# Values' 1x1 products moved ahead of the first convolution, and a fifth buffer of attention weights, in layer 0 of a four-layer network

## The chip, the cores and the metric

The kernel runs on one core of a Trainium2 chip. Its time is the device time in microseconds from the first to the last instruction of the launch, and lower is better. The time before the change is the median of three runs, 4035.57 us (4034.29 to 4037.03).

## The reference, cut to what matters

The network has four layers on x of shape 2 x 128 x 64 x 64 (two samples, 128 channels, 4096 positions), each in the form x + f(groupnorm(x)). Only layer 0 is touched:

```python
xn = biasfree_ln(x, ln1_w)
qkv = conv1x1(xn, w_qkv)                       # 128 -> 5 * 128 channels
qkv = conv3x3_depthwise(qkv, w_dw)             # one 3x3 filter per channel
q1, k1, v, q2, k2 = jnp.split(qkv, 5, axis=1)  # then cut into 4 heads of 32 channels
q1, q2, k1, k2 = map(l2norm_tokens, (q1, q2, k1, k2))
attn1 = softmax(einsum('bhnc,bhmc->bhnm', q1, k1) * temperature)  # 4096 x 4096 per head
out1 = einsum('bhnm,bhmc->bhnc', attn1, v)
attn2 = softmax(einsum('bhnc,bhnd->bhcd', q2, k2) * temperature)  # 32 x 32 per head
out2 = einsum('bhnc,bhcd->bhnd', v, attn2)
out = conv1x1(out1 + out2, w_po)
out = conv1x1(biasfree_ln(out, ln2_w), w_proj) + b_proj
```

## The kernel before, in words

Channels lie on the 128 partitions, positions along the free dimension; everything is float32. Layer 0 (`_layer0`) normalizes the first sample and then does, for each sample b, `convolutions` and `attention`; the end of a sample, `finish` (output products, second normalization, residual), is a generator that runs inside the next sample's convolutions. `_in_order` ties every engine to the order in which the program is written, so the order of the Python statements is the order of each engine's queue. A list written out by hand sets the order around the change.

**Convolutions.** A group (q1, k1, v, q2, k2) is treated in two halves of 32 rows. For each half, `pointwise` (L1586 on) does the 1x1 product: POOL sets the frame's borders to zero (L1588, L1589, L1591), TensorE makes five pieces (L1597), ScalarE copies them from PSUM into a frame of 34 x 66 (four copies, L1604). The 3x3 depthwise filter follows in one of two ways:

- on TensorE (`depthwise`, L1619): 144 products of 32 x 32 blocks with diagonal weights, into two pairs of PSUM banks. This is used for q1, q2, k2 and half 1 of k1: seven blocks n = 0 to 6, in the list `order`. q1 and k1 are then copied by `in_place` (L1639), eight copies each on ScalarE and VectorE; q2 and k2 by `copy` (L1630), one on each engine, into a tile "qk". ScalarE takes sums of squares (L1644).
- on VectorE (`taps`, L1654 and L1656): nine steps over the whole half, one for each tap. This is used for half 0 of k1 and both halves of v: 27 steps. They are dealt out between the blocks by a tuple, one number for each block and one tuple for each sample: (5, 5, 5, 4, 4, 4, 0) for the first, (2, 6, 6, 4, 4, 4, 0) for the second; one more is done ahead.

After block n, `pointwise` for block n + 2 follows on TensorE. The values' `pointwise` are called by `values_of` after blocks 0 and 2. Frames of k1 half 0 and of v share a ring "vpad" of two. After block 2 the norms of q1 and k1 give a scale "sc" (L1766), with which VectorE scales q1 after block 3 (L1770). `products` (L1684, L1694) multiplies q2 by k2 after blocks 4 and 6 (by token, after transposes, copied as "tok" by L1630), `value_tiles` (L1668) turns v after blocks 5 and 6. In the second sample, six of the steps of the first sample's `finish` come after block 0 and the rest after block 1.

**Attention.** There are 8 sweeps (one for each 512 queries) of 32 tiles (128 keys). For each tile TensorE makes scores for four heads (L1858), ScalarE takes the exponential, one bank (L1930) and then three (L1933), into a tile "weights", TensorE multiplies the weights by v two tiles later (L1850), and VectorE adds the weights into running sums (L1881). Four tiles of each sweep start a sum and need no add. A tile of weights is free for ScalarE when both have read it; the ring has four buffers for the first sample and five for the second. At a sweep's end, totals are copied (L1899), turned (L1907) and divided into the result (L1913 to L1916). In the first sample the total and its turned form have tiles of their own, in the second they lie in a tile that is no longer needed. One step in every four tiles goes to side work: the channel attention (whose input is the tile "own", L1775, and the product's copy "folded", L1795), and in the first sample the normalization of the second (tiles "gn", L1545, and "y", L1526).

Of the kernel before, what the change touches and what calls it, by code (L numbers as in the profile page):

```python
# [10 lines left out]
F32 = mybir.dt.float32  # L11
# [5 lines left out]
B, C, H, W = 2, 128, 64, 64  # L17
S = H * W
CH = 512
# [1435 lines left out]
def _layer0(ctx, tc, X, a, cst, worst, there, dram):  # L1455
    nc = tc.nc
    one = ctx.enter_context(tc.tile_pool(name="f0_one", reuse_waits="tile", bufs=1))
    small = ctx.enter_context(tc.tile_pool(name="f0_small", reuse_waits="tile", bufs=2))
# [43 lines left out]
    v = one.tile([128, S], F32, name="v")  # L1502
# [80 lines left out]
    def frame(pool, tag="pad", bufs=2):  # L1583
        return pool.tile([128, H // 2 + 2, W + 2], F32, tag=tag, name=tag, bufs=bufs)

    def pointwise(pad, grp, half):  # L1586

        nc.gpsimd.memset(pad[:, :, 0:1], 0.0)  # L1588
        nc.gpsimd.memset(pad[:, :, W + 1 : W + 2], 0.0)  # L1589
        edge = 0 if half == 0 else H // 2 + 1  # L1590
        nc.gpsimd.memset(pad[:, edge, :], 0.0)  # L1591
        first, to = (0, 1) if half == 0 else (H // 2 - 1, 0)
        for r0, n in ((4 * ROWS, 1), (0, ROWS), (ROWS, 2 * ROWS), (3 * ROWS, ROWS)):
            ps = sp() if n > ROWS else acc(int(r0 == 0)).rearrange("p (o c) -> p o c", o=1)
            for i in range(0, n, ROWS):
                rows = min(ROWS, n - i)
                nc.tensor.matmul(  # L1597
                    ps[:, i // ROWS, : rows * W],
                    w_qkv[:, grp * C : (grp + 1) * C],
                    xn[:, (first + r0 + i) * W : (first + r0 + i + rows) * W],  # L1600
                    start=True,
                    stop=True,
                )
            nc.scalar.copy(  # L1604
                pad[:, to + r0 : to + r0 + n, 1 : W + 1],
                ps.rearrange("p k (h w) -> p (k h) w", w=W)[:, :n, :],
            )
            yield
# [37 lines left out]
    def taps(grp, half, to, pad):  # L1646

        cols = slice(half * S // 2, (half + 1) * S // 2)
        out = to[:, cols].rearrange("p (h w) -> p h w", w=W)
        for t in range(9):  # L1650
            x = pad[:, t // 3 : t // 3 + H // 2, t % 3 : t % 3 + W]
            tap = wd[:, 9 * grp + t : 9 * grp + t + 1]
            if t == 0:
                nc.vector.tensor_scalar_mul(out, x, tap)  # L1654
            else:
                nc.vector.scalar_tensor_tensor(out, x, tap, out, ALU.mult, ALU.add)  # L1656
            yield
# [45 lines left out]
    def convolutions(pool, b, before):  # L1703


        ss = small.tile([128, 2, 4], F32, tag="ss", name="ss")
        ss2 = small.tile([128, 2, 4, 2], F32, tag="ss2", name="ss2")
        gram = None
        order = [(1, 1), (0, 0), (0, 1), (3, 0), (4, 0), (3, 1), (4, 1)]
        kpad = frame(pool, "vpad")  # L1710
        run(pointwise(kpad, 1, 0))
        first = taps(1, 0, k1, kpad)
        frames = [frame(pool) for _ in range(2)]
        run(pointwise(frames[0], *order[0]))
        next(first)
        run(pointwise(frames[1], *order[1]))
        by_vector = first

        def values_of(half):
            pad = frame(pool, "vpad")  # L1720
            run(pointwise(pad, 2, half))
            return taps(2, half, v, pad)

        qk = None
        for n, (grp, half) in enumerate(order):
            ps = depthwise(grp, frames.pop(0))
            following = iter(())
            if n + 2 < len(order):
                frames.append(frame(pool))
                following = pointwise(frames[-1], *order[n + 2])  # L1730
            if grp >= 3:
                if grp == 3:
                    qk = pool.tile([128, 2, 4, CH], F32, tag="qk2", name="qk2", bufs=1)
                for p in range(2):
                    copy(qk[:, grp - 3, 2 * p : 2 * p + 2, :], ps[p])
                run(following)
                for r in range(4):
                    squares(pool, qk[:, grp - 3, r, :], ss2[:, grp - 3, r, half : half + 1])
            else:
                out = (q1, k1)[grp]  # L1740
                in_place(ps, half, out, 0)
                next(following, None)
                in_place(ps, half, out, 1)
                run(following)
                squares_of(pool, out, half, ss[:, grp, :])
            if n == 0:
                by_vector = chain(by_vector, values_of(0))
                for _ in range(FIRST_PART):
                    next(before, None)
            elif n == 1:  # L1750
                run(before)
            if n == 4:
                gram = acc(1)
                run(products(pool, qk, 0, gram))
            elif n == 5:
                run(value_tiles(0))
            elif n == 6:
                run(value_tiles(1))
                run(products(pool, qk, 1, gram))
            if n == 2:  # L1760
                squares_of(pool, k1, 0, ss[:, 1, :])
                by_vector = chain(by_vector, values_of(1))
                nq = inverse_norm(ss[:, 0, :], "nq1")
                nk = inverse_norm(ss[:, 1, :], "nk1")
                sc = small.tile([128, 1], F32, tag="sc", name="sc")
                nc.vector.scalar_tensor_tensor(sc, nq, nk, temp, ALU.mult, ALU.mult)  # L1766
            if n == 3:
                for c in range(0, NCH, 2):
                    cols = slice(c * CH, (c + 2) * CH)
                    nc.vector.tensor_scalar_mul(q1[:, cols], q1[:, cols], sc)  # L1770
            for _ in range(((5, 5, 5, 4, 4, 4, 0), (2, 6, 6, 4, 4, 4, 0))[b > 0][n]):
                next(by_vector, None)

        own = small.tile([128, 4, C], F32, tag="own", name="own", bufs=1)
        nc.vector.tensor_mul(  # L1775
            own,
            gram.rearrange("p (r c) -> p r c", r=4),
            blocks.unsqueeze(1).to_broadcast([128, 4, C]),
        )
        return ss2, own  # L1780
# [58 lines left out]
    def attention(pool, b, side):  # L1839
# [62 lines left out]
        def normalized(qb, first, t):  # L1902
            cols = slice(qb * CH, (qb + 1) * CH)
            turned = xn[:, CH : 2 * CH].rearrange("p (n i) -> p n i", i=32)
            if b == 0:
                turned = pool.tile([128, CH // 32, 32], F32, tag="turned", name="turned", bufs=1)
            nc.vector.transpose(turned.rearrange("p n i -> p (n i)"), t)  # L1907
            if first:
                by_query[qb] = small.tile([128, CH // 32], F32, tag="first", name="first")
                nc.vector.tensor_copy(by_query[qb], turned[:, :, 0])  # L1910
                return
            rec = small.tile([128, CH // 32], F32, tag="rec", name="rec")
            nc.vector.tensor_add(rec, turned[:, :, 0], by_query.pop(qb))  # L1913
            nc.vector.reciprocal(rec, rec)
            nc.vector.transpose(turned, rec.unsqueeze(2).to_broadcast([128, CH // 32, 32]))
            nc.vector.tensor_mul(  # L1916
                q1[:, cols], q1[:, cols], turned.rearrange("p n i -> p (n i)")
            )

        for n in range(last + 1):  # L1920
            kt = n % NQT
            mine, other = 3 * (n % 2), 3 * ((n + 1) % 2)
            three = banks[:, mine : mine + 3, :]
            at["spare"] = [other, other + 1]
            held[n] = pool.tile([128, 4, CH], F32, tag="weights", name="weights", bufs=4 + b)
            scores(n, three)
            total = None
            if len(pending) == 2 and kt in (STARTS[-1] + 1, 1):
                total = totals(banks[:, other + 2, :])
            nc.scalar.activation(held[n][:, 0, :], single, AF.Exp)  # L1930
            if n % 4 == 3:
                next(side, None)
            nc.scalar.activation(held[n][:, 1:, :], three, AF.Exp)  # L1933
            if total:
                emptied(*total)
            if n > 1:
                multiply(n - 2)
            add(n)
            if totalled and kt < 2:
                normalized(*totalled.pop())  # L1940
# [52 lines left out]
    def run(gen):  # L1993
        for _ in gen:
            pass

    def chain(*gens):
        for g in gens:
            yield from g
# [590 lines left out]
```

## Time and profile before

| | us |
|---|---|
| median of the runs | 4035.57 |
| profiled execution, its own time | 4028.9 |
| its span | 4027.1 |
| first sample, convolutions (from the first 1x1 product to the first tile of scores in full flow) | 32.3 to 184.9 |
| first sample, attention | 187.4 to about 769 |
| second sample, convolutions with the first one's finish | 764.1 to 956.7 |
| second sample, attention | 959.2 to about 1517 |
| TensorE busy over the span | 3855.3 |
| VectorE busy over the span | 3198.8 |
| ScalarE busy over the span | 3242.4 |

The profile is one execution; its time is 6.7 us below the median of the runs. A row of a timeline gives the start, the time from the first to the last end of a merged group, engine, line, operation, output and inputs, shapes and count; in square brackets stands the idle time before it and what ended it. A row of waits gives who waited for whom, the total, the number of times and the longest. PE is TensorE, PEld its weight loads, DVE VectorE, ACT ScalarE, POOL GpSimd.

### The profile page before, as it was taken

The page shows a single profiled execution, that of the slowest core. Times are in us where ns is not written, and L with a number is a line of the kernel's source. Part 1 is how long each engine was busy: PE and PEld are TensorE (multiplying, and loading weights), DVE is VectorE, ACT ScalarE, POOL GpSimd, SP SyncE. Part 2 cuts the span into 40 slices and gives each one's busy share as a digit, 9 for nine tenths or more (in the row PEclk, how much of TensorE's full clock was granted, in tenths as well). Part 3 has the DMA queues.
Part 4 walks back from the last instruction along what each step waited for, and adds up shares of the span by engine and source line. Part 5 has one row for each costly group of instructions (what it writes and reads, how often), then busy time and mean ns, then how long its engine had stood idle before and what let it go on. Part 6 is the DMA issues. An engine that isn't in the chain of part 4 may idle for free.

```text
span 4027.1 us, 82181 instructions
## 1 busy us (share of the span) xinstructions
PE 3855.3 (96%) x35214; PEld 1323.1 (33%) x35214; DVE 3198.8 (79%) x3572; ACT 3242.4 (81%) x3955; POOL 79.5 (2%) x145
## 2 busy tenths in 40 slices
PE   7999999989999998997998999999999999999998
PEld 3511222344121114445664332332223222322222
DVE  6699999777999998996667787777777777776666
ACT  5488998736899993216645999999999999999998
POOL 1000000000000001000000000000000000000000
PEclk9999999999999999998998999999999999999999
DMA  1199960000000000004754110110002000110000
GB/s 51 27 197 189 189 95 1 2 2 2 2 2 2 2 2 13 6 3 175 298 217 131 40 40 27 46 53 30 27 24 74 30 27 25 43 48 6 6 6 4
DMA packets 193128, 217.59 MB, mean 54 GB/s; under 512 B 30441, under 2 KB 154345, under 8 KB 188658
## 3 DMA queue, kind: packets, MB, share of 16 engines
q1 hardware_dynamic: 192754, 212.25, 20.6%
q8 instruction: 278, 4.55, 0.5%
q14 instruction: 96, 0.79, 0.1%
HBM read 178.64 MB, written 98.57 MB: 69 GB/s over the span
## 4 chain that ended last, share of the span: by engine, by line
PE 68%; DVE 5%; issue 2%; ACT 1%; POOL 0%; SPq 0%; DMA 0%; POOLq 0%; DVEq 0%; ACTq 0%
PE ps_acc L2305 25%; PE ps_s L2282 18%; PE ps L1850 6%; PE ps L1858 6%; PE ps_bank L710 2%; PE ps_z L1008 2%; DVE e L950 2%; PE ps_t L640 1%; PE ps_bank L590 1%; PE ps_bank L1062 1%; PE ps_bank L681 1%; PE ps_acc L2209 1%; PE ps_acc L2163 1%; PE ps_pe L925 1%; DVE sums L1881 1%
## 5 line engine op out<-in xcount | busy, mean ns | idle before, releaser
L2296 ACT ACTIVATE weights<-ps_s 128x1024 f32<-128x1024 f32 x1920 | 1780.9, 1066 | 75.0 <-PE ps_s L2282 74.9
L2305 PE MATMUL ps_acc<-weights,vt 128*32 128x512 f32 x8192 | 1091.9, 605 | 0.0
L1881 DVE TENSOR_TENSOR sums<-sums,weights 128x2048 f32<-128x2048 f32 x384 | 854.9, 2285 | 7.8 <-ACT weights L1933 5.6
L2282 PE MATMUL ps_s<-q,k 64*128 64x512 f32 x4096 | 830.8, 470 | 3.5 <-DMA k<-stack 2.4
L1933 ACT ACTIVATE weights<-ps 128x1536 f32<-128x1536 f32 x512 | 740.7, 1447 | 8.5 <-PE ps L1858 8.5
L2282 PEld LDWEIGHTS ps_s<-q,k 64*128 64x128 f32 x4096 | 349.3, 184 | 934.3 <-ACT weights L2296 808.8
L1858 PE MATMUL ps<-q,k 32*64 32x512 f32 x8192 | 575.0, 613 | 12.5 <-ACT weights L1930 11.8
L1850 PE MATMUL ps<-weights,vt 128*32 128x512 f32 x4096 | 545.0, 604 | 0.0
L2254 DVE SCALAR_TENSOR_TENSOR exp_z<-exp_z,exp_m 128x1024 f32<-128x1024 f32 x384 | 469.0, 1221 | 9.3
L1930 ACT ACTIVATE weights<-ps 128x512 f32<-128x512 f32 x512 | 306.6, 599 | 88.3 <-PE ps L1858 33.5
L2238 DVE TENSOR_SCALAR exp_i<-ps_s 128x1024 int32<-128x1024 f32 x128 | 156.7, 1225 | 215.3 <-PE ps_s L2282 215.1
L1858 PEld LDWEIGHTS ps<-q,k 32*64 32x64 f32 x8192 | 120.6, 130 | 442.5 <-ACT weights L1930 393.4
L2305 PEld LDWEIGHTS ps_acc<-weights,vt 128*32 128x32 f32 x8192 | 162.4, 108 | 308.9 <-issue 308.1
L1850 PEld LDWEIGHTS ps<-weights,vt 128*32 128x32 f32 x4096 | 84.5, 108 | 391.1 <-issue 378.1
L662 DVE SCALAR_TENSOR_TENSOR X<-g,w,X 128x2048 f32<-128x2048 f32 x84 | 197.4, 2351 | 2.6
L1881 DVE TENSOR_TENSOR sums<-weights 128x2048 f32<-128x2048 f32 x64 | 145.8, 2289 | 32.7 <-ACT weights L1933 31.9
L2258 DVE SCALAR_TENSOR_TENSOR weights<-exp_z,exp_i 128x1024 f32<-128x1024 f32 x128 | 156.8, 1225 | 15.6 <-DVE exp_z L2254 0.5
L2254 DVE SCALAR_TENSOR_TENSOR exp_z<-exp_m 128x1024 f32<-128x1024 f32 x128 | 155.9, 1218 | 0.0
L1008 PE MATMUL ps_z<-w_ri,e 128*32 128x128 f32 x2048 | 137.5, 409 | 14.6 <-DVE e L950 12.4
L1619 PE MATMUL ps<-pad,diag 32*32 32x512 f32 x4032 | 144.0, 611 | 4.0 <-ACT vt L1630 3.7
L950 DVE TENSOR_SCALAR e<-ps_pe 32x136 f32<-32x136 f32 (+1 forms) x352 | 104.4, 297 | 4.9
L1619 PEld LDWEIGHTS ps<-pad,diag 32*32 32x32 f32 x4032 | 84.3, 104 | 59.3 <-issue 21.4
(310 smaller groups left out, 2955.6 us busy)
## 6 DMA issues: line engine op xcount, KB each, us to landing
w_ri<-w_r SPq DMA_DIRECT2D x16, 2112.0 KB, 7.9
w_ri<-w_i SPq DMA_DIRECT2D x16, 2112.0 KB, 13.5
stack<-qs SPq DMA_DIRECT2D x64, 256.0 KB, 2.1
q<-stack SPq DMA_DIRECT2D x128, 128.0 KB, 2.5
k<-stack SPq DMA_DIRECT2D x128, 128.0 KB, 2.6
stack<-ks SPq DMA_DIRECT2D x32, 256.0 KB, 2.2
w_r<-in_L_conv_kr_w SPq DMA_DIRECT2D x15, 528.0 KB, 12.6
w_r<-in_L_conv_kr_x SPq DMA_DIRECT2D x15, 528.0 KB, 12.8
```

What stands on the lines that cost most here:

```text
L662: nc.vector.scalar_tensor_tensor(xi, g[:, i : i + H // 2, j : j + W], w8[:, s : s + 1], xi, ALU.mult, ALU.add)
L1008: nc.tensor.matmul(out.rearrange("p (n f o) -> p n f o", n=2, f=2), e[:, s, 2 * j : 2 * j + 2, :].rearrange("p f x -> p (f x)"), w.rearran ...
L1619: nc.tensor.matmul(ps[r // 2][to, r % 2, :].rearrange("p (h w) -> p h w", w=W), diag[rows, grp, t, :], pad[rows, y0 : y0 + ROWS, t % 3 : t ...
L1850: nc.tensor.matmul(out[rows, :], lhs(rows), w[:, j, :], start=first, stop=stop)
L1858: nc.tensor.matmul(bank[64 * h : 64 * h + 64, :], k1[rows, kt * 128 + 64 * h : kt * 128 + 64 * h + 64], q1[rows, qb * CH : (qb + 1) * CH], ...
L1881: nc.vector.tensor_add(parts[p].rearrange("p j c -> p (j c)"), t.rearrange("p j c -> p (j c)"), w.rearrange("p j c -> p (j c)"),)
L1930: nc.scalar.activation(held[n][:, 0, :], single, AF.Exp)
L1933: nc.scalar.activation(held[n][:, 1:, :], three, AF.Exp)
L2254: nc.vector.scalar_tensor_tensor(z, x, n, m, ALU.add, ALU.mult)
L2282: nc.tensor.matmul(ps[j // 2][:, j % 2, :], g.k[kt // 4][rows, j // 2, keys], g.q[qb][rows, j // 2, :], start=True, stop=True,)
L2296: nc.scalar.activation(w[0], ps[p], AF.Exp)
L2305: nc.tensor.matmul(g.ac[32 * j : 32 * j + 32, :], g.vt[:, kt, j // 2, i : i + 2, :].rearrange("p a d -> p (a d)"), w[:, i, :], start=(at = ...
```

## The change

Both halves' 1x1 products of v now come before block 0, after those of k1 half 0 and of blocks 0 and 1, with two taps on VectorE after each of the four (eight ahead in all). The tuples that deal the taps are new. k1's frame lies in the ring of "qk" (which is first used at block 3), so the values' two frames have the ring "vpad" to themselves. The first sample's attention has five buffers of weights. To make room, "own" moves into the ring of "gn" (one buffer) and "turned" into the ring of "y" (two).

```diff
         order = [(1, 1), (0, 0), (0, 1), (3, 0), (4, 0), (3, 1), (4, 1)]
-        kpad = frame(pool, "vpad")
+        kpad = pool.tile([128, 8 * CH], F32, tag="qk2", name="kpad", bufs=1)
+        kpad = kpad[:, : (H // 2 + 2) * (W + 2)].rearrange("p (h w) -> p h w", w=W + 2)
         run(pointwise(kpad, 1, 0))
         first = taps(1, 0, k1, kpad)
         frames = [frame(pool) for _ in range(2)]
-        run(pointwise(frames[0], *order[0]))
-        next(first)
-        run(pointwise(frames[1], *order[1]))
-        by_vector = first
+        by_vector = [first]
+
+        def ahead():
+            for _ in range(2):
+                next(first)
 
         def values_of(half):
             pad = frame(pool, "vpad")
             run(pointwise(pad, 2, half))
-            return taps(2, half, v, pad)
+            by_vector.append(taps(2, half, v, pad))
+
+        for n in range(2):
+            run(pointwise(frames[n], *order[n]))
+            ahead()
+        for n in range(2):
+            values_of(n)
+            ahead()
+        by_vector = chain(*by_vector)
...
             if n == 0:
-                by_vector = chain(by_vector, values_of(0))
                 for _ in range(FIRST_PART):
...
                 squares_of(pool, k1, 0, ss[:, 1, :])
-                by_vector = chain(by_vector, values_of(1))
...
-            for _ in range(((5, 5, 5, 4, 4, 4, 0), (2, 6, 6, 4, 4, 4, 0))[b > 0][n]):
+            for _ in range(((3, 3, 3, 2, 4, 4, 0), (0, 2, 4, 4, 4, 5, 0))[b > 0][n]):
                 next(by_vector, None)
 
-        own = small.tile([128, 4, C], F32, tag="own", name="own", bufs=1)
+        own = cp.tile([128, 4, C], F32, tag="gn", name="own", bufs=1)
...
-                turned = pool.tile([128, CH // 32, 32], F32, tag="turned", name="turned", bufs=1)
+                turned = cp.tile([128, CH // 32, 32], F32, tag="y", name="turned")
...
-            held[n] = pool.tile([128, 4, CH], F32, tag="weights", name="weights", bufs=4 + b)
+            held[n] = pool.tile([128, 4, CH], F32, tag="weights", name="weights", bufs=5)
```

## The prediction

> **What bounds the kernel now.** I read the page first, then the TensorE, VectorE and ScalarE timelines of the two convolution stages (32 to 183 us for the first sample, 764 to 955 us for the second), then busy times by stretch and the waits of the two attention stages between and after them. The page says that the whole is a TensorE chain, so what counts is where TensorE stands still.
>
> ```profile
> PE 3855.3 (96%) x35214; PEld 1323.1 (33%) x35214; DVE 3198.8 (79%) x3572; ACT 3242.4 (81%) x3955; POOL 79.5 (2%) x145
> ...
> PE 68%; DVE 5%; issue 2%; ACT 1%; POOL 0%; SPq 0%; DMA 0%; POOLq 0%; DVEq 0%; ACTq 0%
> ```
>
> Attention, first sample and second, by stretch (length, then busy PE, PEld, DVE, ACT, POOL, clock, DMA):
>
> ```profile
> 187.40:765.20 577.80, 564.91 (x6439) 117.18 (x6439) 544.81 (x387) 520.96 (x566) 16.27 (x16) 1.00 0.73 121
> 959.20:1514.30 555.10, 551.72 (x6381) 109.71 (x6381) 529.28 (x307) 508.76 (x542) 11.93 (x2) 1.00 0.01 2
> ```
>
> TensorE idles 577.8 - 564.9 = 12.9 us in the first, with four weight buffers, and 555.1 - 551.7 = 3.4 us in the second, which has five already. The waits of the first name the chain:
>
> ```profile
> ACT weights L1930 <- DVE sums L1881: 18.8, 26, 1.9
> ...
> PE ps L1858 <- ACT weights L1930: 10.6, 17, 1.7
> ```
>
> ScalarE cannot write the next exponentials until VectorE's add has read the buffer, and TensorE then waits for ScalarE. In the second sample no wait of L1930 on DVE is listed.
>
> The convolution stage is a sequence of depthwise blocks (L1619, 9.7 us each) with 1x1 products (L1597, 3.9 us) between. First sample, TensorE:
>
> ```profile
> 57.81 3.92 PE L1597 MATMUL ps<-xn,w_qkv 128*128 128x64 f32 x10
> 64.89 3.92 PE L1597 MATMUL ps<-xn,w_qkv 128*128 128x64 f32 x10 [3.16 <-ACT pad L1604]
> 68.75 9.75 PE L1619 MATMUL ps<-pad,diag 32*32 32x512 f32 x288
> 78.43 3.92 PE L1597 MATMUL ps<-xn,w_qkv 128*128 128x64 f32 x10
> 82.28 1.04 PE L1619 MATMUL ps<-pad,diag 32*32 32x512 f32 x2
> 83.49 10.50 PE L1619 MATMUL ps<-pad,diag 32*32 32x512 f32 x286 [0.17 <-ACT q L1639]
> 93.92 3.92 PE L1597 MATMUL ps<-xn,w_qkv 128*128 128x64 f32 x10
> 101.00 5.81 PE L1597 MATMUL ps<-xn,w_qkv 128*128 128x64 f32 x10 [3.16 <-ACT pad L1604]
> ```
>
> The second L1597 row after a block is the values' product. The gap between blocks is 10.9 us with it (57.8 to 68.75) and 12.8 us (93.9 to 106.7, the next block's start), but 3.9 us plus a wait of about 2 for the copies without it (78.4, 83.5).
>
> Second sample, VectorE and then TensorE:
>
> ```profile
> 850.92 14.28 DVE L1656 SCALAR_TENSOR_TENSOR k<-vpad,wd,k 128x2048 f32<-128x2048 f32 x6
> 865.23 5.62 DVE L1639 COPY q<-ps 32x512 f32<-32x512 f32 x8
> ```
>
> ```profile
> 859.83 3.92 PE L1597 MATMUL ps<-xn,w_qkv 128*128 128x64 f32 x10
> 866.91 3.07 PE L1597 MATMUL ps<-xn,w_qkv 128*128 128x64 f32 x8 [3.15 <-ACT pad L1604]
> 876.07 2.08 PE L1597 MATMUL ps<-xn,w_qkv 128*128 128x512 f32 x2 [6.09 <-ACT vpad L1604]
> ```
>
> Six taps hold VectorE until 865.2, 5.4 us after the block's end at 859.8. ScalarE's squares need that copy, the values' copies are queued behind the squares, and TensorE waits 6.09 us more.
>
> [...] the stretch 101.0 to 106.7, after 3.16 us idle, has a granted clock of 0.72, while 64.89, after the same idle, runs at full speed. [...] 26 ScalarE waits with four buffers, none with five.
>
> **The change part by part.**
>
> *Five buffers.* Nothing is added. Per buffer the ring gives one more tile of slack, and a tile takes 2.04 us (ScalarE's steady spacing, 207.45 to 209.49). The longest ScalarE wait is 1.9 us, so each of the 26 is covered. VectorE has room: 544.8 busy of the 568 that remain. What is late next is TensorE itself, with the second sample's 3.4 us of idle time. Gain 12.9 - 3.4 = 9.5; I keep back 0.5 for the sweep 475.5 to 551.4, where the next sample's normalization makes VectorE 71.0 busy beside TensorE's 72.3. **-9.0 us**; bounds -10.5 and -4 (half of it moves on).
>
> *Two tiles moved.* "own" enters the ring of "gn" (last read by TensorE before 33 us, and for the second sample inside the first attention); "folded", its successor, is a copy of the product that reads it. "turned" enters the ring of "y"; in the built order its transpose waits for ScalarE alone. Cost 0, hidden by the product itself; without that cover one wait of about 1 us in each of eight sweeps.
>
> *Values first, first sample.* Two 1x1 products move ahead of block 0. Each costs the spacing seen there, 4.66 us (39.61 to 44.27): TensorE 3.92, the rest its wait for ScalarE's copies. Block 0 starts 9.3 later, at 57.4, and ends at 67.1. GpSimd's six border memsets (about 0.16 each) go ahead too, to about 3 us, where it idles until 13.2. VectorE does eight taps meanwhile, 1.29 + 7 x 2.38 = 17.9, from 39.6 to 57.5, in its idle time. Removed: the values' gaps. What is late next is the release of the PSUM banks by the eight copies on each of ScalarE and VectorE: 5.8 us after a block's end (78.43 to 84.23). So block to block is 15.5, as between 78.4 and 93.9: block 1 ends 82.6, block 2 98.1, block 3 113.6 (before 116.4), 2.8 earlier. Then VectorE binds: the scale "sc" is ready 12.8 after block 2 (93.9 to 106.7), 110.9; three taps follow (7.1), so its copy of block 3 ends at 118.0 + 1.2 = 119.3, and block 4, queued behind it on TensorE, starts at 119.3, not 117.5. Before, it started at 120.3. Everything later keeps its offsets: four taps at the end instead of three still finish before block 6. **-1.0 us**; bounds -3 and +3.
>
> *Second sample.* Block 0 again 9.3 later, 787.8 to 797.5. The first part of the last sample's finish begins when the banks are free, 5.1 later (802.6), its statistics 2.0 after that, and block 1 follows 17.1 after them: 821.7, against 818.1. Its remainder takes the 22.3 us it took (827.8 to 850.1), so block 2 is 853.7 to 863.4. Now only two taps stand before its copies, which are on time; block 3 ends 15.5 later, at 878.9 (before 889.7): 10.8 earlier. Four taps after "sc" (876.3 + 9.5) put VectorE's copy of block 3 at 885.8 to 887.0, and block 4 waits for it: 887.0 to 896.7, before 903.2: 6.5 earlier. Five taps at the end finish at about 938.2, against block 6's end at 937.5: 0.6 back. **-5.9 us**; bounds -9 and +1.
>
> *Clock.* Two new idle stretches before block 4 (1.8 and 4.2 us). About half of such stretches were followed by a slow one that cost 1.6 to 1.9 (101.0; 160.99 to 172.2, a block of 11.3). I take **+1.0**; 0 to 3.5.
>
> Sum: -9.0 - 1.0 - 5.9 + 1.0 = -14.9. Against the profiled execution's own 4028.9 us (span 4027.1, 1.8 around it) this is 4014.0. The median of the runs, 4035.57, lies 6.7 above the profiled time; I carry that over: 4020.7.
>
> **Rivals.** (A) The above, 4020.7. (B) VectorE becomes the attention's bound in the three sweeps that carry the normalization (busy 68.8 to 71.0 of 72.3), and stalls return later: attention -4, total -9.9, 4025.7. For it: the near equality; against it: four tiles of each sweep need no add. (C) Only one of the two halves pays, say VectorE's late copy ahead of block 4 takes back what the convolutions win and 2 more: -9 + 2 = -7, 4028.6, which is no change by the bound I use (0.2%, 8 us, about what a measurement of this kernel can tell from no change). (D) Slower: the gap after blocks 0 and 2 is not set by the values' product but by something that stays (the 3.16 us in which ScalarE is copying, and its squares). Then 2 x 9.3 = 18.6 is added and only VectorE's 5.4 us of lateness and the 9 of attention go, of which the cold clock takes 3.5 and rival B's loss 5 back: 18.6 - 5.4 - 9 + 8.5 = +12.7, 4048.3. It decides from a gap of about 9 us after those blocks. Against it: 78.4 to 84.2 shows the bare gap.
>
> **Numbers.** A 0.62, B 0.16, C 0.14, D 0.08. A is faster, B nearly always (0.13 of 0.16), C is no change: faster 0.75, same 0.17, slower 0.08. Range: bounds of A below, -10.5 - 3 - 9 = -22.5, 4013; above, B and C with a little over, 4030. D and a small tail are left out.
>
> **What would show it.** In the first attention, L1930's waits on DVE gone and TensorE idle under 5 us of some 568. In the convolutions, blocks 1, 2 and 3 ending 15.5 apart; block 4 released by VectorE's copy of qk; no L1597 row waiting for vpad after block 0. Wrong would be: a gap over 7 us after block 0 or 2; L1930 still waiting on sums; DVE waits of y or turned on PE.

## The result, and the profile after

The median falls from 4035.57 to 4012.48 us (five runs each), a ratio of 0.9944 with a 95% interval of 0.9932 to 0.9957. That is -23.1 us where -14.9 was forecast, and 0.5 us below the range. The profiled execution, however, went from 4028.9 to 4012.5, -16.4, close to the -14.9 of the sum. So there are two questions: whether each step of the sum happened as worked out, and what the other 6.7 us are.

The page of the changed kernel: TensorE is as busy as before, in a span that is 16.4 shorter, and has a larger share of the last chain.

```profile
PE 3857.8 (96%) x35214; PEld 1318.5 (33%) x35214; DVE 3197.1 (80%) x3572; ACT 3247.0 (81%) x3955; POOL 86.2 (2%) x145
...
PE 81%; DVE 7%; issue 4%; ACT 3%; POOL 0%; DMA 0%; SPq 0%; POOLq 0%; ACTq 0%; DVEq 0%
```

Attention of the first and of the second sample, by stretch, and the waits of the first:

```profile
189.50:757.30 567.80, 562.66 (x6439) 116.18 (x6439) 543.78 (x387) 522.36 (x564) 22.66 (x13) 1.00 0.72 123
944.50:1498.50 554.00, 550.94 (x6373) 109.34 (x6373) 528.18 (x305) 509.03 (x542) 11.93 (x2) 1.00 0.01 2
```

```profile
ACT weights L1938 <- PE ps L1866: 17.8, 38, 1.3
...
PE ps L1866 <- ACT weights L1938: 1.8, 4, 1.2
...
ACT weights L1938 <- DVE sums L1889: 0.4, 1, 0.4
```

TensorE's idle time in the first attention went from 12.9 to 567.8 - 562.7 = 5.1 us, a little above the 5 us that the prediction had named. The 26 waits of ScalarE for the adds (18.8 us) have become one of 0.4, and ScalarE now waits for TensorE's scores, as in the second sample (18.7 us in 42 waits there).

The first sample's convolutions, TensorE. Blocks 0 to 3 end where the next L1597 row begins:

```profile
69.66 3.92 PE L1597 MATMUL ps<-xn,w_qkv 128*128 128x64 f32 x10
73.51 1.04 PE L1619 MATMUL ps<-pad,diag 32*32 32x512 f32 x2
74.72 10.48 PE L1619 MATMUL ps<-pad,diag 32*32 32x512 f32 x286 [0.17 <-ACT k L1639]
85.14 3.92 PE L1597 MATMUL ps<-xn,w_qkv 128*128 128x64 f32 x10
...
115.98 3.92 PE L1597 MATMUL ps<-xn,w_qkv 128*128 128x64 f32 x10
119.83 1.05 PE L1619 MATMUL ps<-pad,diag 32*32 32x512 f32 x4
121.80 9.72 PE L1619 MATMUL ps<-pad,diag 32*32 32x512 f32 x284 [0.91 <-DVE qk L1630]
```

One 1x1 product stands between blocks in place of two. Block 1 follows block 0 by 85.14 - 69.66 = 15.5 us, and block 4 is released by VectorE's copy of qk, as forecast. The second sample, VectorE and then TensorE, shows the same wait, larger:

```profile
867.07 9.51 DVE L1656 SCALAR_TENSOR_TENSOR v<-vpad,wd,v 128x2048 f32<-128x2048 f32 x4
876.61 1.22 DVE L1630 COPY qk<-ps 128x1024 f32<-128x1024 f32 x1
```

```profile
869.76 3.92 PE L1597 MATMUL ps<-xn,w_qkv 128*128 128x64 f32 x10
873.61 1.05 PE L1619 MATMUL ps<-pad,diag 32*32 32x512 f32 x4
877.88 12.35 PE L1619 MATMUL ps<-pad,diag 32*32 32x512 f32 x284 [3.22 <-DVE qk L1630]
```

Four taps hold the copy until 876.6 while block 3 had ended at 869.8. TensorE idles 3.22 us, and the block after it takes 12.35, at a granted clock of 0.76, where 9.7 is usual.

### The profile page after: what moved, and what is told of

Read it like the earlier page. It is cut to its first block, busy times and chain, and to the rows that moved or that the text cites. A ratio compares the mean times of both kernels' runs of the same rounds, so it can differ in the third digit from the quotient of the medians.

```text
span 4010.7 us, 82168 instructions
## 1 busy us (share of the span) xinstructions
PE 3857.8 (96%) x35214; PEld 1318.5 (33%) x35214; DVE 3197.1 (80%) x3572; ACT 3247.0 (81%) x3955; POOL 86.2 (2%) x145
## 4 chain that ended last, share of the span: by engine, by line
PE 81%; DVE 7%; issue 4%; ACT 3%; POOL 0%; DMA 0%; SPq 0%; POOLq 0%; ACTq 0%; DVEq 0%
PE ps_acc L2313 25%; PE ps_s L2290 19%; PE ps L1858 11%; PE ps L1866 11%; PE ps_bank L710 2%; PE ps_z L1008 2%; DVE sums L1889 2%; PE ps L1619 2%; DVE e L950 1%; PE ps_t L640 1%; PE ps_bank L590 1%; PE ps_bank L1062 1%; PE ps_bank L681 1%; PE ps_acc L2171 1%; PE ps_acc L2217 1%
## 5 line engine op out<-in xcount | busy, mean ns | idle before, releaser
L1619 PEld LDWEIGHTS ps<-pad,diag 32*32 32x32 f32 x4032 | 86.2, 104 | 69.2 <-issue 21.1
## 6 DMA issues: line engine op xcount, KB each, us to landing
w_r<-in_L_conv_kr_x SPq DMA_DIRECT2D x15, 528.0 KB, 12.5
```

Of the source, the lines that this page charges most:

```text
L1619: nc.tensor.matmul(ps[r // 2][to, r % 2, :].rearrange("p (h w) -> p h w", w=W), diag[rows, grp, t, :], pad[rows, y0 : y0 + ROWS, t % 3 : t ...
```

## The experiments

Two theories stood against each other. The first: the profile that I worked from was a lucky execution, with less clock lost than usual, and the median holds clock losses that the change removes. The rival: the missing time lies in the attention, or timed executions differ from profiled ones in some constant way. All ratios are against the kernel before on the same chip.

**The kernel before, profiled again (c1).** No edit.

> The kernel before, once more, to see how far one profiled execution lies from the median. Theory 1 (the profiled execution of before, 4028.9, was a lucky one, and the change is worth what its stages show plus that luck): this profile is a few us longer than the first, near 4034, by a slow stretch of the clock somewhere, and the stages of layer 0 last as they did within 2 us. Theory 2 (profiled executions of before are always about 6 us shorter than its timed ones, because the timed ones lose clock in the gaps that the change closes): the profile is again near 4029 and the timed median near 4035.

Measured: its profile takes 4041.4 us, 12.5 more than the first. Over 37 executions the kernel before lies between 4026 and 4045, median about 4037. TensorE in c1, after block 0:

```profile
59.42 3.92 PE L1597 MATMUL ps<-xn,w_qkv 128*128 128x64 f32 x10
66.50 6.85 PE L1597 MATMUL ps<-xn,w_qkv 128*128 128x64 f32 x10 [3.16 <-ACT pad L1604]
```

This is the pair of rows shown for before at 57.81 and 64.89: the same idle time of 3.16 us, but the values' product takes 6.85 us instead of 3.92. Block 1 starts 3 us later for it. In the second sample the same row has 7.07. The granted clock of the stretch 67.0 to 73.3 is 0.57; in the first profile it was 1.00 there. So the first profile was a lucky one, as theory 1 says; the constant difference between profiled and timed executions that theory 2 supposes is out. Theory 1 was wrong on the size (12.5 us, not about 5) and in holding that layer 0's stages last as before within 2 us: they are 3.3 and 4.3 longer. That clock is lost in the gaps which the change closes was theory 2's own reason, and it is what these rows show for this gap, with 0.57 behind it.

**Further profiles of both kernels (c3, c4, c5, c2).** No edit.

> One more profile of the kernel before, for the length of its convolution stages (first sample 152.7 and 156.0 so far, second 192.6 and 196.9) and of the values' product in the gap after block 0 (3.92, 6.85; 3.92, 7.07). Theory (the clock falls in that gap in some executions): again between these, and a long product wherever the stage is long. Rival (the first profile was the ordinary one): 152.7 and 192.6 within 0.5.

> As the look before it: theory, stages between 152 and 156 and between 192 and 197, long where a values' product is long; rival, 152.7 and 192.6 within 0.5.

> One more profile of the changed kernel: both theories, 151.7 to 152.7 in the first stage and 184 to 186 in the second, blocks 1, 2 and 3 of the first sample 15.4 to 15.5 apart.

> The changed kernel once more. Both theories: median 4012 within 2 us, ratio 0.994 to before. Theory 1: its profiled execution lies anywhere within 4 us of the median. Theory 2: at the median, and the stages of layer 0 as in the first profile within 1 us.

Measured, in us (stages from the first 1x1 product to the scores in full flow; attention from there to the next sample's first 1x1 product):

| profile | time | values' product after block 0, samples 1, 2 | stage 1 | attention 1 | stage 2 |
|---|---|---|---|---|---|
| before, first | 4028.9 | 3.92, 3.92 | 152.7 | 579.2 | 192.6 |
| before, c4 | 4029.2 | 3.92, 3.92 | 152.7 | 579.2 | 192.5 |
| before, c3 | 4036.2 | 5.62, 5.62 | 152.8 | 579.2 | 195.4 |
| before, c1 | 4041.4 | 6.85, 7.07 | 156.0 | 579.2 | 196.9 |
| after, first | 4012.5 | none there | 152.6 | 569.9 | 185.8 |
| after, c2 | 4014.6 | none there | 152.7 | 569.9 | 185.9 |
| after, c5 | 4011.5 | none there | 151.7 | 569.9 | 186.2 |

So c4 came out as the rival had it, like the first profile; c3 came out as the theory had it in the second sample (195.4), but in the first its stage is not longer although the product is. c2 and c5 lie within 0.2 us of what was expected. The two rows side by side, from c4 and from c3:

```profile
65.20 3.92 PE L1597 MATMUL ps<-xn,w_qkv 128*128 128x64 f32 x10 [3.16 <-ACT pad L1604]
```

```profile
65.02 5.62 PE L1597 MATMUL ps<-xn,w_qkv 128*128 128x64 f32 x10 [3.16 <-ACT pad L1604]
```

The four profiled executions of before sort by that product; the two with 3.92 twice are the quickest. The product after block 2 of the first sample, also behind 3.16 us, does not vary: it takes 5.8 us in all four. In c3 stage 1 made it good later (block 6 took 1.6 less than in c4), so a long product is a sign of a long execution and not its whole cost. The second run of the change (c2) gave a median of 4013.95, ratio 0.9943 (0.9929 to 0.9957). The mean clock of each of 81 executions of before goes with its time: at 0.980 their mean is 4040.2 us (25 of them), at 0.981 4036.8 (22), at 0.982 4031.8 (17), at 0.983 4029.9 (7), at 0.984 4026.4 (3). The executions of after that c2 timed, which lie at 0.983 to 0.986, span 4010 to 4017.

**Five buffers alone (e1).**

```diff
-        own = small.tile([128, 4, C], F32, tag="own", name="own", bufs=1)
+        own = cp.tile([128, 4, C], F32, tag="gn", name="own", bufs=1)
-                turned = pool.tile([128, CH // 32, 32], F32, tag="turned", name="turned", bufs=1)
+                turned = cp.tile([128, CH // 32, 32], F32, tag="y", name="turned")
-            held[n] = pool.tile([128, 4, CH], F32, tag="weights", name="weights", bufs=4 + b)
+            held[n] = pool.tile([128, 4, CH], F32, tag="weights", name="weights", bufs=5)
```

> The attention half alone: five buffers, own in the ring of gn, turned in that of y; convolutions as before. My sum says -9.0 (the two profiles show -9.3): median about 4026, waits of ScalarE's first exponential on VectorE's sums gone in the first attention, TensorE idle there under 5 us. Rival (the missing 7 us of the forecast lie in the attention): -15, about 4020.

Measured: 4025.05 against 4036.49, ratio 0.9977 (0.9966 to 0.9988), about -9. The attention in its profile takes 569.9 us, as in the changed kernel; TensorE's idle time there, expected under 5 us, is 568.3 - 562.5 = 5.8. Its waits in the first attention:

```profile
PE ps L1858 <- ACT weights L1930: 2.1, 6, 1.2
...
ACT weights L1930 <- DVE sums L1881: 0.4, 1, 0.4
```

The attention half is worth what the sum said, and the rival's -15 lies outside the interval.

**Values first alone (e2).** The convolution part of the diff, with "own", "turned" and four buffers as before.

> The convolution half alone: values' products first and taps dealt anew; four buffers in the first sample's attention. My sum says -1.0 - 5.9 + 1.0 = -5.9 (the two profiles show -1.1 and -6.8): median about 4028 to 4030. Rival (the missing 7 us lie here, in clock that timed executions of before lose in the gaps which the change closes): -13, about 4022.

Measured: 4023.24, ratio 0.9970 (0.9956 to 0.9983), about -12, with times between 4019.5 and 4025.7. The forecast was -5.9, just outside the interval (-7 to -18). The profile's stages take 151.7 and 184.2 us, 1.8 and 10.1 less than the mean of the four profiles of before. The missing time is in this half, and the spread of the times narrows with this half too: 6 us in seven executions, where before has 19 in 23. The two halves' ratios add up to about -21; the whole change has -23 by its ratio.

**Taps dealt anew, values' products left in their places (e3).** This splits the half. The frame of k1 moves too, which the new tuple needs, since k1's taps now end later.

```diff
-        kpad = frame(pool, "vpad")
+        kpad = pool.tile([128, 8 * CH], F32, tag="qk2", name="kpad", bufs=1)
+        kpad = kpad[:, : (H // 2 + 2) * (W + 2)].rearrange("p (h w) -> p h w", w=W + 2)
...
-            for _ in range(((5, 5, 5, 4, 4, 4, 0), (2, 6, 6, 4, 4, 4, 0))[b > 0][n]):
+            for _ in range(((5, 5, 5, 4, 4, 4, 0), (2, 3, 5, 6, 5, 5, 0))[b > 0][n]):
```

> Before, with only the second sample's taps dealt anew, (2, 3, 5, 6, 5, 5, 0) in place of (2, 6, 6, 4, 4, 4, 0), and k1's frame in the ring of qk, which that needs; the values' products stay after blocks 0 and 2. Theory (the values' gaps and the clock lost in them are the larger part of the convolution half): VectorE's copies of block 2 of the second sample are on time, the gap from block 2 to block 3 falls from 18.2 to the 12.75 of the first sample, -5.4, of which later taps give 1 to 2 back: about -4, median 4032 to 4033; the clock still drops in the gaps, so single times stay spread over some 15 us. Rival (the lateness of the taps was the whole matter): -13, median 4023, with a narrow spread.

Measured: 4026.89 against 4038.13, ratio 0.9977 (0.9970 to 0.9985), about -9, between theory and rival. TensorE after block 2 of the second sample:

```profile
874.24 3.07 PE L1597 MATMUL ps<-xn,w_qkv 128*128 128x64 f32 x8 [3.18 <-ACT pad L1604]
878.93 1.13 PE L1597 MATMUL ps<-xn,w_qkv 128*128 128x512 f32 x2 [1.63 <-ACT vpad L1604]
879.99 9.75 PE L1619 MATMUL ps<-pad,diag 32*32 32x512 f32 x288
```

Block 3 in the first profile of before, behind the row of 876.07:

```profile
878.07 11.70 PE L1619 MATMUL ps<-pad,diag 32*32 32x512 f32 x288
```

The wait of 6.09 us is 1.63, the two products after it take 1.13 instead of 2.08, and block 3 takes 9.75 where four profiles of before have 10.4 to 11.7. In the first of these the granted clock was 0.50 over the two products and 0.81 over the block. My -4 left out that clock: where the 6 us of idle time ended, the slow block behind it ended too. This does not account for all of the -9. The profile of this run is one of its longer executions (4031.2), with 5.62 and 7.07 us for the values' product after block 0; its second stage, 191.3 us, is 5.6 shorter than that of c1, which also has 7.07 there. The other 3 us of the median are not found in a stage. The times still reach from 4022.6 to 4041.9, and the gap after block 0 stays, with its long products. The rest of the half, about 3 us by the two ratios, would belong to moving the values; the intervals of the two overlap, so this last number is weak.

**Late taps with the values ahead (e4).**

```diff
-            for _ in range(((3, 3, 3, 2, 4, 4, 0), (0, 2, 4, 4, 4, 5, 0))[b > 0][n]):
+            for _ in range(((3, 3, 3, 2, 4, 4, 0), (0, 6, 4, 3, 3, 3, 0))[b > 0][n]):
```

> The changed kernel with the second sample's taps as late as before: (0, 6, 4, 3, 3, 3, 0) in place of (0, 2, 4, 4, 4, 5, 0). Theory: VectorE ends its six taps 4.2 us after block 2, so block 3 and with it block 4 start 4.2 later, and the end gets back 0.6: +3.6 to +4, about 4017.5, plus up to 3 where a longer idle of TensorE drops the clock. Rival (the dealing of the taps does not matter once the values are ahead): 4013.5.

Measured: 4017.67, 3.7 above c2's 4013.95, which was taken on another chip; ratio to before 0.9954 (0.9941 to 0.9967), an interval that overlaps c2's. VectorE after block 1 of the second sample, where block 2 had ended at 851.95:

```profile
846.61 9.51 DVE L1656 SCALAR_TENSOR_TENSOR v<-vpad,wd,v 128x2048 f32<-128x2048 f32 x4
856.13 5.62 DVE L1639 COPY q<-ps 32x512 f32<-32x512 f32 x8
```

The taps are 4.2 us late, as worked out, and the median agrees, but in part by luck, since the path in the profile differs from the expectation. Block 3 ends 5.8 later than in after (it took 11.37 in its last part). Block 4 ends only 0.5 later, since here it took 9.7 instead of 12.35, and of the stage's 3.4 us 1.4 come back right behind it, where the products up to block 5 take 16.1 us in place of 14.7, and the rest later. So the lateness of the copy is shown, and its price of 3.7 us is not.

**Fewer taps after block 2 (e5).** The version that the profile after suggests: VectorE idles before block 2 and is late after it.

```diff
-            for _ in range(((3, 3, 3, 2, 4, 4, 0), (0, 2, 4, 4, 4, 5, 0))[b > 0][n]):
+            for _ in range(((3, 4, 2, 2, 4, 4, 0), (0, 4, 2, 4, 4, 5, 0))[b > 0][n]):
```

> The changed kernel with fewer taps after block 2, where VectorE holds block 4 up, and more after block 1, where it idles 4 to 6 us: (3, 4, 2, 2, 4, 4, 0) and (0, 4, 2, 4, 4, 5, 0) in place of (3, 3, 3, 2, 4, 4, 0) and (0, 2, 4, 4, 4, 5, 0). Theory: block 4 follows its 1x1 product at once; first sample -2 (the 0.91 us and the copies' tail), second -4.2, and up to 2.6 more there for the clock that drops after 3.22 us of idle time (a block of 12.35 instead of 9.7): -6 to -8, about 4006. Rival (something else, ScalarE or the products after block 4, takes the time up): within 2 us of 4013.

Measured: 4004.9, between 4003.2 and 4008.0; ratio to before 0.9920 (0.9907 to 0.9933). That is 9 us below the changed kernel's 4013.95 in c2, on another chip, and the two ratios differ by as much; their intervals overlap only between 0.9929 and 0.9933. Second sample, TensorE after blocks 2 and 3:

```profile
863.26 3.92 PE L1597 MATMUL ps<-xn,w_qkv 128*128 128x64 f32 x10
867.11 9.76 PE L1619 MATMUL ps<-pad,diag 32*32 32x512 f32 x288
```

No wait, and 9.76 instead of 12.35. The stages take 148.1 and 179.1, against a mean of 152.3 and 186.0 for after: -4.2 and -6.9. The second is as expected (-4.2 and -2.6); in the first it came to about 2 more than I had counted: block 4 ran unbroken (9.77 us), and the stretch of products after it took 14.7 us in place of the first after profile's 16.2. Together that is 11.1, more than the 9 of the medians; after layer 0, where the two kernels are the same, this profile took 4.3 us longer than the mean of after.

**Unneeded products in the gaps of before (e6).** After blocks 0 and 2, ahead of the values' product, three products whose result nothing reads:

```diff
+        def fill(out):
+            for i in range(3):
+                nc.tensor.matmul(out, w_qkv[:, :C], xn[:, i * CH : (i + 1) * CH], start=True, stop=True)
...
             if n == 0:
+                fill(ps[0][:, 0, :])
                 by_vector = chain(by_vector, values_of(0))
...
+                fill(ps[0][:, 0, :])
                 by_vector = chain(by_vector, values_of(1))
```

> The kernel before, with unneeded work added: three products of 128x512 into a bank that is already read, in TensorE's idle 3.16 us ahead of the values' 1x1 products, after blocks 0 and 2 of both samples (about 0.96 us each, 2.9 in all, so nothing waits for them). Nothing reads their result. Theory (idle time there lets the clock fall, and the missing 7 us of my forecast are the clock): no values' product is longer than 3.92 any more, where the profiles of before have 3.92 to 7.07; -3 to -6 in the median, 4032 to 4035 against 4038, and a narrower spread than the 18 us of before. Rival (the clock falls for another reason, such as load, or the gaps cost the same anyhow): no change or slower, the long products stay.

```profile
60.44 3.92 PE L1597 MATMUL ps<-xn,w_qkv 128*128 128x64 f32 x10
64.20 2.74 PE L1721 MATMUL ps<-xn,w_qkv 128*128 128x512 f32 x6
67.52 3.92 PE L1597 MATMUL ps<-xn,w_qkv 128*128 128x64 f32 x10 [0.59 <-ACT pad L1604]
```

Measured: 4033.95 against 4037.17, ratio 0.9994 (0.9985 to 1.0003). The rows after block 0 are as the theory has them: idle 0.59 instead of 3.16, and 3.92 in both samples. After block 2 of the second sample, where 6.07 us of waiting stay, the last two instructions still take 2.07. The median moved as expected, but the interval holds no change, so the medians do not decide. One profile cannot either, since two of four profiles of before have 3.92 as well. The spread says more: it is 10.8 us against 15.4, and 9 of the 17 executions of before on this chip took longer than the longest of the 13 with the products (4036.9). This comparison was made after the result, and the profiled execution itself is no quick one (4036.5): its stages of layer 0 take 152.1 and 192.5 us, but what follows layer 0 took 6.7 longer than in the first profile of before. A second thing seen here: after block 2 of the first sample, where the product took 5.81 in before and now takes 3.07 for its first eight instructions and 1.12 for the last two, the gap stays at 12.75, because ScalarE's copies, behind its squares, end it (1.62 us of waiting for vpad). There the slow product had cost nothing.

## Why the prediction missed: the steps held, the clock term and the carried difference did not

**Attention, -9.0.** Right: -9.3, from 579.2 to 569.9, the same in every profile of the two kernels. The idle time fell by 7.8 and not quite to that of the second sample (5.1 us, forecast 3.4 with 0.5 kept back); the rest is that the same 6439 instructions show less busy time (562.7 against 564.9), and why is open. Rival B, which had -4, is out. Moving the two tiles cost nothing to be seen.

**First sample, -1.0.** Right in its steps up to block 4. The first product of the changed profile started 1.5 us later, and the two after it 2.5; with that taken off, block 0 ends at 67.1 (forecast 67.1), block 3 at 113.4 (113.6) and block 4 at 128.9 (129.0). Between the two first profiles the stage shows only -0.1, because its first products were slower in the changed one (2.34 us for 1.35 in the first row of L1597); its mean over the profiles went from 153.5 to 152.3, -1.2.

**Second sample, -5.9.** The steps are right within 1.4 us. Counted from the stage's first product, as forecast and as measured: block 2 ends at 99.3 and 98.1, block 3 at 114.8 and 113.6, block 4 at 132.6 and 134.0. Two errors of the sum offset each other here. The first part of the last sample's finish was to wait for the banks, 5.1 us after block 0; it began 3.8 after it (789.53 to 793.29), so everything up to block 3 came 1.2 to 1.3 earlier. Block 4 then took 2.6 longer than I had counted. The stage went from 192.6 to 185.8 between the two first profiles, -6.8, but from a mean of 194.3 to 186.0 over all, -8.3.

**Clock, +1.0. This step failed.** I counted only the idle stretches that the change adds, and did find one: 3.22 us, then a block of 12.35 (12.40 in c2, 11.06 in c5). I left out those that it takes away, because the one after block 0 had cost nothing in the profile before me: "while 64.89, after the same idle, runs at full speed". I had rows with both outcomes, and took one execution for the price; c1 and c3 have 5.62 to 7.07 us in that place. Without this term I had -6.9 for the two convolution stages; the means of the seven profiles give -9.5. So by difference the term was about -2.6, an estimate, where I had +1.0 and a range of 0 to 3.5 that left no room for a gain.

**The 6.7 us carried over. This failed for the same reason.** "The median of the runs, 4035.57, lies 6.7 above the profiled time; I carry that over." The first profile of before was among the quickest executions: of 81 between 4026 and 4045 us, six took 4028.9 or less. So the difference was no constant of the measurement but time that most executions lose, and in the changed kernel it is gone: its profile, 4012.48, is its median. The change removes only part of the places where that time is lost. Of the 12.5 us that c1 took longer than the first profile, 7.6 lie in the two convolution stages, but 3.5 after layer 0, in code that did not change, and 1.4 before the first product; of the 7.3 of c3 it is 3.0 in the stages and 4.1 after layer 0. Counted against the profiled execution, as the sum was, 4014.0 was forecast and 4012.5 measured.

Adding the means of the table, -1.2 - 9.3 - 8.3 = -18.8. The means of the profiles' times differ by 21.1, the medians by 23.1, the interval of the ratio reaching from -17 to -27; the four profiles of before average 4034.0, below the median of the 81 executions, 4037.4. About 2 us by the profiles lie outside these stages, and no run tells where they come from; times after layer 0 differ by up to 8 us between profiles of kernels that are the same there.

Why the clock falls behind an idle stretch in one execution and not in another was not shown. The traces have the outcomes: the same 3.16 us ahead of the same work, followed by 3.92 us (at a granted clock of 1.00 in the first profile of before), by 5.62 or by about 7 (6.85 at 0.57 in c1). After block 2 of the first sample 3.16 us were followed by 5.8 in all four profiles of before, at 0.72 in the first; and the 1.84 us ahead of block 6 were followed by 11.32 in the first, at 0.85, and in c4, but by 9.7 in c1 and c3. That the idle stretch is the cause is argued from these rows, from e3 and from e5; e6, which tested it alone, agrees in the sign of the median, which is not clear of zero, and in the narrower spread.

Rival C is out, since both halves pay (e1, e2). Rival D is out: the bare gap gives 15.5 us from block to block.

## What to carry to other kernels

Where an engine copies out what TensorE waits for, place its other work ahead of the copy only as far as it is idle there. Here four taps ahead of VectorE's copy made TensorE wait 3.22 us, and with two (e5) it did not wait; moving three taps across one block (e5: one in the first sample, two in the second) gave about as much as the attention's fifth buffer, 9 us, and with no resource at all. Price an idle stretch of TensorE from several executions: what followed it here was slow in some and not in others (3.92 to 7.07 us). Where a wait of 6.09 us became 1.63 (e3), the slow block behind it went too (9.75 us in place of 10.4 to 11.7); where another engine ended the gap anyhow, as after block 2 of the first sample (e6), the quicker product gained nothing, 12.75 us with both. And compare profiled with profiled and median with median: a gap between one profile and the median is a finding about the kernel, to be explained before it is carried over.

## What was not expected of the hardware

The same product of ten matrix instructions after 3.15 to 3.17 us of idle time took 3.92, 5.62, 6.85 or 7.07 us. The granted clock of a whole execution and its time went together over 81 executions of one kernel, from a mean of 4042 us at 0.979 to 4026 at 0.984. And work that nothing needs, put into an idle stretch (e6), did not make the kernel slower: 0.9994 (0.9985 to 1.0003).
